# A recurrent kernel's head: rows of x turned by the array, input weights in chunks, biases loaded on all partitions

## The chip, the cores and the metric

The kernel runs on one core of one Trainium2 chip. A core has a matmul array with its weight loader (PE and PEld in the profile), VectorE (DVE), ScalarE (ACT), GpSimd (POOL) and a queue engine (SP), and 16 DMA engines that carry all its transfers. The metric is the device time of one execution in microseconds; all times below are microseconds unless marked otherwise.

## The reference

A gated recurrent layer over 128 steps of a batch of 64, with 512 inputs and 512 states, added to its input:

```
x: (64, 128, 512), h0: (64, 512)
Wz, Wr, Wh: (1024, 512)   # upper 512 rows meet x, lower 512 meet the state
Wp: (512, 512)

step t:
  z = sigmoid([x_t, h] @ Wz + bz)
  r = sigmoid([x_t, h] @ Wr + br)
  c = tanh([x_t, r * h] @ Wh + bh)
  h_new = (1 - z) * h + z * c
  y_t = h_new
  h = tanh(h_new @ Wp + bp)  if (t + 1) % 4 == 0 and t < 127  else h_new
out = x + y
```

All of it is in 32-bit floats.

## The kernel before

The work falls into two parts. The state part is serial: at each step the gates r, z and the candidate multiply the turned state (`hT`, `rhT`) by the state weights `wh[R]`, `wh[Z]`, `wh[H_]` (the lower halves), and at each fourth step by `wp`. The x part does not depend on the state: products of x with `wx`, the upper halves of the three weights. From step 4 on, the x part is computed for groups of four steps together by a scheme of fewer, pre-summed products (`batch`, with sums of weights in `tt`, `tw`, `d5`, `din` and sums of x in `s12r` and others); the first four steps are done one by one (`plain`).

A batch of 64 is handled as two halves of 32 (`h` = 0, 1). A product of one k (one of K = 4 blocks of 128 inputs) and one half is two matmuls of a 128x32 stationary tile against 256 columns (`products`, L222 is their matmul); a *unit* below is one k for both halves. Results of the x part gather in the PSUM tiles `scratch` q, r, a, x, y; `add_bias` (DVE, L437) adds the bias and writes `cp`, and `seed` (ScalarE, L398) copies `cp` into the PSUM of a gate (`rec`, `rec_z`) before the state's products are added there.

The order on each engine is the order in which the program issues the instructions; nothing reorders them. Two generators, `half(0)` and `half(1)`, walk over the steps, and a queue of x units fills the gaps between the gates (`fill`, with the numbers in `HEAD`, `PLACES`, `TAIL`). `both(n)` runs n units for both halves at once, `now` queues units and runs them.

The head stands before these generators. The array begins with idle matmuls on zeros (`idle`, L212). Meanwhile SP and ScalarE issue the loads: x of steps 0 to 3 in quarters (`load_step`, L112, pieces of 512 bytes), the input weights of r in two parts and of z and the candidate in one each (`load_wx`, L117), and later the state weights in quarters of 256 KB, each to 32 partitions, from both queues (`load_wh`, L98). x is turned by DVE (`join_x`, L264). The three biases come as rows through GpSimd's queue (L130), are spread over the partitions by matmuls against ones (`spread`, L194) and copied by ScalarE into `bias_x` (L202). GpSimd then waits on a copy `held` (L142), loads h0 (L144), forms the difference of the two halves of the biases (`bias_d`, L659), and begins the sums of weights (`sum_inner`, L318 to L321; `sum_outer`, L302 to L306). DVE does some of these sums itself (`sum_inner` of 1 and 2, `sum_outer_1` at L310), and turns h0 into `hT` (L251).

Each load takes a semaphore out of a small ring, so that a load waits, in the queue that issues it, for an earlier load that used the same semaphore; loads behind it in that queue wait too. GpSimd's loads have semaphores of their own.

Of the kernel before, what the change touches and what calls it, by code (L numbers as in the profile page):

```python
# [18 lines left out]
def kernel(  # L19
# [18 lines left out]
    S = 2  # L38
# [29 lines left out]
    ones = const.tile([1, V], F32, name="ones")  # L68
    nc.gpsimd.memset(ones, 1.0)
# [14 lines left out]
    bias_row = tw_all.rearrange("p a b -> p (a b)")[0:1, : 3 * H].rearrange("p (i n) -> p i n", i=3)  # L84
# [11 lines left out]
    def load_w(wt, w, k0=0, k1=K, engs=(nc.sync, nc.sync)):  # L96
        for q in (0, 2, 1, 3):
            engs[q // 2].dma_start(  # L98
                out=wt[part(q), k0:k1, :],
                in_=w[q * P + k0 * V : q * P + k1 * V, :].rearrange("(k e) n -> e k n", e=V),  # L100
            )
# [8 lines left out]
    def load_step(t, engs=both_queues):  # L110
        for q in (0, 2, 1, 3):
            engs[q // 2].dma_start(  # L112
# [3 lines left out]
    def load_wx(i, k0, k1):  # L116
        nc.sync.dma_start(  # L117
# [8 lines left out]
    load_step(0)  # L126
    load_wx(R, 0, 2)
    load_step(1, (nc.scalar, nc.scalar))
    for i, b in enumerate((br, bh, bz)):
        nc.gpsimd.dma_start(out=bias_row[:, i, :], in_=b.rearrange("(o n) -> o n", o=1))  # L130
    load_wx(R, 2, K)

    dummy = const.tile([1, 1], F32, name="dummy")
    nc.scalar.activation(dummy, ones[:, 0:1], AF.Sigmoid)

    for i in (Z, H_):
        load_wx(i, 0, K)

    for t in (2, 3):
        load_step(t, (nc.sync, nc.sync))  # L140
    held = const.tile([1, 1], F32, name="held")
    nc.gpsimd.tensor_copy(held, wx[0:1, 2, R, 0:1])  # L142
    for h in range(S):
# [3 lines left out]
        )  # L147

    def load_wh(i):
        load_w(wh[i], gates_in[i][D:], engs=both_queues)  # L150
# [39 lines left out]
    def spread(bank, rows, which):  # L190
        bank = bank.rearrange("p (i d j) -> p i d j", i=2, d=2)
        for h in range(S):
            for c in range(2):
                nc.tensor.matmul(  # L194
                    bank[part(2 * h + c), 0 : len(which)],
                    lhsT=ones,
                    rhs=quarters(bias_row[:, rows])[:, c],
                    start=True,
                    stop=True,
                )  # L200
        for j, i in enumerate(which):
            nc.scalar.copy(  # L202
                bias_x[:, :, :, i, :].rearrange("p n d u -> p d n u"),
                bank[:, j].rearrange("p d (n u) -> p d n u", n=C),
            )
# [52 lines left out]
    def join_x(g, i):  # L258
# [8 lines left out]
        )  # L267

# [160 lines left out]
    def banks(t):  # L429
        first, second = scratch[:2] if t % 2 == 0 else scratch[2:4]  # L430
        rooms = (first[:, : S * J], first[:, S * J :], second[:, : S * J])
# [11 lines left out]
    def plain_unit(t, e, k, start, end=None, gates=()):  # L443
# [4 lines left out]
        second = H_ if t == T - 1 else Z  # L448
# [554 lines left out]
```

## Time and profile before

| | |
|---|---|
| median of 3 runs | 1262.05 (1261.39 to 1263.48) |
| profiled execution | 1259.52, of which the span of the instructions 1257.6 |
| PE busy | 1250.6 (99%), 25960 matmul records |
| DVE, ACT, POOL busy | 805.5 (64%), 837.9 (67%), 891.5 (71%) |
| read from HBM, written to it | 40.11 MB, 16.78 MB |
| share of the 16 DMA engines in the first two slices of 31 us | 8 and 3 tenths |

Engine rows of the timeline give start, length, engine, line, operation, tiles written and read, and in brackets the idle time before with what ended it. A matmul of 32-bit floats is two records. In the chain of work each piece is what the end of the span was waiting for at that time. The row of a DMA issue gives the queue, the count, KB of each and the median time from issue to landing. Several matmuls of 32 columns run beside each other in the array, so the records' lengths overlap, and the time between starts counts.

### The profile page before, as it was taken

To read this page: it belongs to the slowest core of one execution; us is meant where nothing else is said; L and a number is where in the kernel's file an instruction comes from. 1 tells how busy PE (TensorE), PEld (TensorE's weight loads), DVE (VectorE), ACT (ScalarE), POOL (GpSimd) and SP (SyncE) were. 2 spreads that over 40 slices of the span, in tenths; PEclk is the share of its full clock that TensorE was granted. 3 is DMA by queue.
4 is the path that set the end of the run, shared out by engine and by line. 5 is a ranking of instruction groups with operands and counts; after the bars stand their busy time and mean duration, and the time that the engine had idled before them with its cause. 6 is when DMAs were issued, how large, how long until landed. Compare 5 with 4: busy or idle time off the path is not lost.

```text
span 1257.6 us, 60730 instructions
## 1 busy us (share of the span) xinstructions
PE 1250.6 (99%) x25960; PEld 1162.1 (92%) x25960; DVE 805.5 (64%) x2173; ACT 837.9 (67%) x2685; POOL 891.5 (71%) x1031
## 2 busy tenths in 40 slices
PE   9999999999999999999999999999999999999998
PEld 4899999999999999999999999999999999999975
DVE  4666666666666666666666666666666666666545
ACT  2566666767666666766666667667676666676665
POOL 3988877776876778767788676786777777677530
PEclk9999999999999999999999999999999999999999
DMA  8311112121121110211211111111111111111010
GB/s 240 91 28 45 49 41 53 36 54 39 34 53 48 41 47 26 53 53 37 53 29 43 53 43 47 38 47 41 53 37 49 40 37 53 42 48 37 9 42 23
DMA packets 113232, 60.82 MB, mean 48 GB/s; under 512 B 12836, under 2 KB 109348, under 8 KB 112964
## 3 DMA queue, kind: packets, MB, share of 16 engines
q1 hardware_dynamic: 111268, 55.00, 16.4%
q8 instruction: 205, 3.36, 1.1%
q10 hardware_dynamic: 1440, 1.80, 0.6%
q14 instruction: 63, 0.52, 0.1%
q0 software_dynamic: 256, 0.14, 0.1%
HBM read 40.11 MB, written 16.78 MB: 45 GB/s over the span
## 4 chain that ended last, share of the span: by engine, by line
PE 98%; DMA 1%; issue 1%; DVE 0%; SPq 0%; POOLq 0%; POOL 0%; ACT 0%; ACTq 0%
PE rec L222 44%; PE rec_z L222 16%; PE scratch_r L222 14%; PE scratch_q L222 11%; PE scratch_a L222 5%; PE scratch_x L222 4%; PE scratch_y L222 4%; DMA wx<-in_L_cond_Wr_dram 0%; SPq L821 0%; DMA xr<-in_x_dram 0%; DMA out_dram<-xr 0%; PE scratch_x L194 0%; DVE z L912 0%; POOLq L998 0%; POOL xr L811 0%
## 5 line engine op out<-in xcount | busy, mean ns | idle before, releaser
L222 PE MATMUL rec<-wh,rhT 128*32 128x256 f32 x4096 | 376.3, 379 | 0.0
L222 PE MATMUL rec<-wh,hT 128*32 128x256 f32 x3072 | 282.6, 379 | 0.0
L222 PE MATMUL rec_z<-wh,hT 128*32 128x256 f32 x3072 | 282.5, 379 | 0.0
L222 PEld LDWEIGHTS rec<-wh,rhT 128*32 128x32 f32 x4096 | 249.6, 110 | 21.1 <-ACT rec L398 1.2
L248 ACT ACTIVATE scratch_r<-rec 64x128 f32<-64x128 f32 x512 | 128.2, 250 | 138.3 <-PE rec L222 63.7
L398 ACT COPY rec<-cp 64x256 f32<-64x256 f32 x512 | 190.6, 372 | 19.9 <-DVE cp L437 0.4
L222 PEld LDWEIGHTS rec<-wh,hT 128*32 128x32 f32 x3072 | 187.4, 110 | 14.7 <-issue 1.8
L222 PEld LDWEIGHTS rec_z<-wh,hT 128*32 128x32 f32 x3072 | 193.8, 110 | 7.2
L248 ACT ACTIVATE rec_z<-rec_z 64x128 f32<-64x128 f32 x488 | 122.2, 250 | 90.1 <-PE rec_z L222 78.6
L248 ACT ACTIVATE c<-rec 64x128 f32<-64x128 f32 x512 | 139.7, 273 | 60.4 <-PE rec L222 48.8
L811 POOL TENSOR_TENSOR xr<-xr,h 128x256 f32<-128x256 f32 x127 | 93.2, 734 | 91.6 <-DVE h L925 91.6
L575 POOL TENSOR_TENSOR mb<-mb,mb 128x768 f32<-128x768 f32 x58 | 106.3, 1833 | 66.8 <-DVE mb L541 66.8
L575 POOL TENSOR_TENSOR cp<-mb,mb 128x768 f32<-128x768 f32 x76 | 139.2, 1831 | 9.5 <-DVE mb L541 5.8
L575 POOL TENSOR_TENSOR cp<-mb 128x768 f32<-128x768 f32 x46 | 84.2, 1831 | 57.0 <-ACT rec_z L398 55.5
L222 PE MATMUL scratch_r<-tw,s 128*32 128x192 f32 x928 | 120.9, 326 | 0.0
L514 ACT COPY cq<-scratch_q 128x384 f32<-128x384 f32 x212 | 102.1, 482 | 19.3 <-PE scratch_q L222 17.8
L531 DVE TENSOR_TENSOR cx<-scratch_r,cx 128x384 f32<-128x384 f32 x106 | 59.1, 558 | 84.1 <-PE scratch_r L222 66.8
L222 PE MATMUL scratch_q<-tt,s 128*32 128x192 f32 x928 | 103.7, 326 | 0.0
L873 DVE SCALAR_TENSOR_TENSOR keep<-rec_z,h 128x256 f32<-128x256 f32 x91 | 38.7, 425 | 95.6 <-ACT rec_z L248 94.6
L537 DVE TENSOR_TENSOR mb<-scratch_q,cx 128x384 f32<-128x384 f32 x106 | 59.1, 558 | 62.4 <-ACT cq L514 62.4
L853 DVE TENSOR_TENSOR rh<-scratch_r,h 128x128 f32<-128x128 f32 x192 | 56.1, 292 | 61.2 <-ACT scratch_r L248 61.2
L222 PE MATMUL rec<-wp,hT 128*32 128x256 f32 x992 | 91.5, 379 | 0.1
(188 smaller groups left out, 3846.5 us busy)
## 6 DMA issues: line engine op xcount, KB each, us to landing
out_dram<-xr SPq DMA_DIRECT2D x249, 64.0 KB, 1.8
xr<-in_x_dram SPq DMA_DIRECT2D x248, 64.0 KB, 2.1
xs<-in_x_dram SPq DMA_DIRECT2D x240, 64.0 KB, 2.0
wx<-in_L_cond_Wr_dram SPq DMA_DIRECT2D x2, 512.0 KB, 5.1
wx<-in_L_cond_Wz_dram SPq DMA_DIRECT2D x1, 1024.0 KB, 5.9
wx<-in_L_cond_Wh_dram SPq DMA_DIRECT2D x1, 1024.0 KB, 8.2
wp<-in_L_cond_Wp_dram SPq DMA_DIRECT2D x4, 256.0 KB, 5.3
wh<-in_L_cond_Wr_dram ACTq DMA_DIRECT2D x2, 256.0 KB, 3.8
```

Of the source, the lines that this page charges most:

```text
L222: nc.tensor.matmul(ps[part(2 * h + c)], lhsT=left, rhs=rhs(c), start=start, stop=True, skip_group_check=True,)
L248: nc.scalar.activation(dst[ts(d, 2 * V)], gate_ps(i, h)[ts(h, 2 * V), d, :], func)
L398: nc.scalar.copy(gate_ps(i, h)[rows].rearrange("p d (c n) -> p d c n", c=C), G[t][rows, :, :, i, :].rearrange("p c d n -> p d c n"),)
L514: nc.scalar.copy(c[:, :nm], ps[:, :nm])
L531: nc.vector.tensor_add(T2[what][:, :nm], r_ps[:, :nm], T2[what][:, :nm])
L537: nc.vector.tensor_add(blocks(1, 1), runs(q_ps[:, :nm]), runs(T2[what][:, :nm]))
L575: nc.gpsimd.tensor_add(dst, a, b)
L811: nc.gpsimd.tensor_add(xr[g][:, j], xr[g][:, j], h_new)
L853: nc.vector.tensor_mul(rh[:, h, :], r_, h_old[:, h, :])
L873: nc.vector.scalar_tensor_tensor(out=keep[:, part, :], in0=z_[:, part, :], scalar=1.0, in1=h_old[:, part, :], op0=ALU.subtract, op1=ALU.mult,)
```

## The change

- The array has an identity of 64x64 (`ident`, made by GpSimd). x of steps 0 and 1 is loaded as 64 rows of 2 KB (`load_rows`), turned by four transposes of the array for each step (`turn_rows`), and copied out of PSUM by DVE. The quarters of these two steps that the residual needs are loaded later, among the state weights of the candidate.
- r's input weights come in four loads of one k each (the first by ScalarE's queue), those of z and of the candidate in two each. The products of steps 0 and 1 are ordered so that each chunk of r is used for both steps when it is there; z's and the candidate's go by halves of k. The candidate's products of steps 0 and 1 get PSUM of their own (`scratch[4]`).
- The biases are loaded by twelve loads through GpSimd's queue directly to all partitions; the matmuls of `spread` are gone, `place_bias` is its copy by ScalarE. h0 comes between the biases of r and z. The copy `held` in front of them now waits for z's first half.
- The state weights are issued by SP alone, those of z with the quarters of x of step 3 between, those of the candidate with x of steps 0 and 1.
- 24 and 4 idle matmuls in place of 48; eight units ahead of step 0 in place of nine, with one more in step 0; on DVE `sum_outer_1` and the turn of x of step 3 stand ahead of the candidate's `add_bias`, and `bias_d` comes last on GpSimd before the sums; the turns of steps 4 and 5 and their sums move to the end of step 0.

```diff
-    def load_x(tile_, t0, n, j=0, engs=(nc.sync, nc.sync)):
-        for h in range(S):
-            for q in (0, 2, 1, 3):
-                engs[q // 2].dma_start(
+    def load_x(tile_, t0, n, j=0, hs=range(S), qs=(0, 2, 1, 3)):
+        for h in hs:
+            for q in qs:
+                nc.sync.dma_start(
...
-    load_step(0)
-    load_wx(R, 0, 2)
-    load_step(1, (nc.scalar, nc.scalar))
-    for i, b in enumerate((br, bh, bz)):
-        nc.gpsimd.dma_start(out=bias_row[:, i, :], in_=b.rearrange("(o n) -> o n", o=1))
-    load_wx(R, 2, K)
+    def load_rows(t, eng):
+        eng.dma_start(out=x_rows[:, ts(t, D)], in_=x[:, t, :])
+
+    load_rows(0, nc.sync)
+    load_wx(R, 0, 1, nc.scalar)
+    load_rows(1, nc.scalar)
+    for k in range(1, K):
+        load_wx(R, k, k + 1)
+    for k in (0, 2):
+        load_wx(Z, k, k + 2)
...
-    for i in (Z, H_):
-        load_wx(i, 0, K)
-
-    for t in (2, 3):
-        load_step(t, (nc.sync, nc.sync))
+    load_step(2)
+    for k in (0, 2):
+        load_wx(H_, k, k + 2)
     held = const.tile([1, 1], F32, name="held")
-    nc.gpsimd.tensor_copy(held, wx[0:1, 2, R, 0:1])
+    nc.gpsimd.tensor_copy(held, wx[0:1, 0, Z, 0:1])
+
+    def load_bias(i, b):
+        for q in range(NQ):
+            nc.gpsimd.dma_start(
+                out=bias_in[part(q), i],
+                in_=b.rearrange("(o d c j) -> c o d j", o=1, d=2, c=2)[q % 2].broadcast_to(
+                    [V, S, J]
+                ),
+            )
+
+    load_bias(R, br)
     for h in range(S):
         nc.gpsimd.dma_start(
             out=h_init[:, h, :],
             in_=h0[ts(h, V), :].rearrange("b (q j) -> q b j", q=NQ),
         )
+    load_bias(Z, bz)
+    load_bias(H_, bh)
...
+    def place_bias(i):
+        nc.scalar.copy(
+            bias_x[:, :, :, i, :].rearrange("p n d u -> p d n u"),
+            bias_in[:, i].rearrange("p d (n u) -> p d n u", n=C),
+        )
...
+    def turn_rows(t, bank):
+        if 0 not in xT:
+            xT[0] = xtp.tile([P, Q4, C, P], F32, tag="xT", name="xT_0")
+        for k in range(K):
+            nc.tensor.transpose(
+                bank[:, ts(k, B)],
+                x_rows[:, ts(t, D)].rearrange("b (p k) -> b k p", k=K)[:, k],
+                ident,
+            )
+        nc.vector.tensor_copy(xT[0][:, t].rearrange("p c n -> p (c n)"), bank[:, : K * B])
...
-    idle(48)
-    join_x(0, 0)
-    now(first[R][0])
-    join_x(0, 1)
-    now(first[R][1])
-    now(first[Z][0])
-    for i in (1, 2):
-        sum_inner(i, nc.vector, slice(0, 2))
-    spread(scratch[3], slice(0, 2), (R, H_))
+    idle(24)
+    turn_rows(0, scratch[4])
+    idle(4)
+    now(first[R][0][:1])
+    turn_rows(1, scratch[3])
+    for t, k in ((0, 1), (1, 0), (1, 1), (0, 2), (1, 2), (0, 3), (1, 3)):
+        now([first[R][t][k]])
+    for half_k in (slice(0, 2), slice(2, K)):
+        for t in range(2):
+            now(first[Z][t][half_k])
     load_wh(R)
-    now(first[Z][1])
+    for q in (0, 2, 1, 3):
+        load_step(3, (q,))
+        load_wh(Z, (q,))
+    for q in (0, 2, 1, 3):
+        load_x(xr[0], 0, 2, hs=(0,), qs=(q,))
+        load_wh(H_, (q,))
+    load_x(xr[0], 0, 2, hs=(1,))
+    sum_inner(1, nc.vector, slice(0, 2))
+    join_x(0, 2)
+    place_bias(R)
     for t in range(2):
         add_bias(t, (R,))
     for h in range(S):
         seed(R, 0, h)
-    spread(scratch[4], slice(2, 3), (Z,))
-    nc.gpsimd.tensor_sub(bias_d, bias_x[:, 1], bias0)
-    load_wh(Z)
+    sum_inner(2, nc.vector, slice(0, 2))
+    place_bias(Z)
     for t in range(2):
         add_bias(t, (Z,))
     seed(Z, 0, 0)
-    load_wh(H_)
-    join_x(0, 2)
     hT = new_T("hT", "hT_init")
     for h in range(S):
         turn(hT[:, h, :], h_init[:, h, :])
+    for half_k in (slice(0, 2), slice(2, K)):
+        for t in range(2):
+            now(first[H_][t][half_k])
+    sum_outer_1(nc.vector)
+    join_x(0, 3)
+    place_bias(H_)
+    for t in range(2):
+        add_bias(t, (H_,))
     for i in (1, 2):
         sum_inner(i, nc.vector, slice(2, 3))
-    now(sum(first[H_], []))
-    for t in range(2):
-        add_bias(t, (H_,))
-    join_x(0, 3)
-    sum_outer_1(nc.vector)
+    nc.gpsimd.tensor_sub(bias_d, bias_x[:, 1], bias0)
     nc.gpsimd.tensor_copy(held, d5[0:1, 1, 0, 0, 0:1])
...
-    both(9)
+    both(8)
...
         if t == 0:
+            join_x(1, 0)
+            join_x(1, 1)
+            sum_raw12(1)
             sum_outer(2)
             sum_outer(4)
...
-                yield from fill(2 * K - 3, h)
+                yield from fill(2 * K - 2, h)
...
-                if t == 0:
-                    join_x(1, 0)
-                    join_x(1, 1)
-                    sum_raw12(1)
```

More of the change, by code (lines that the diff above doesn't have):

```diff
@@ L67 @@
     nc.vector.memset(zeros, 0.0)
-    ones = const.tile([1, V], F32, name="ones")
-    nc.gpsimd.memset(ones, 1.0)
+    ident = const.tile([B, B], F32, name="ident")
+    make_identity(nc, ident)
     wx = const.tile([P, K, 3, H], F32, name="wx")
@@ L108, in new_xr, with load_step, load_wx @@
         xr[g] = xrp.tile([P, Q4, S, J], F32, tag="xr", name=f"xr_{g}")
-    def load_step(t, engs=both_queues):
-        for q in (0, 2, 1, 3):
-            engs[q // 2].dma_start(
+    def load_step(t, qs=(0, 2, 1, 3)):
+        for q in qs:
+            nc.sync.dma_start(
                 out=xr[0][part(q), t], in_=x[:, t, ts(q, J)].rearrange("(h b) u -> b h u", h=S)
             )
-    def load_wx(i, k0, k1):
-        nc.sync.dma_start(
+    def load_wx(i, k0, k1, eng=nc.sync):
+        eng.dma_start(
             out=wx[:, k0:k1, i, :],
@@ L188, in quarters @@
         return v.rearrange("p n (d c j) -> p c n d j", d=2, c=2)
[L190 to L205, printed above, removed]
+    def place_bias(i):
+        nc.scalar.copy(
+            bias_x[:, :, :, i, :].rearrange("p n d u -> p d n u"),
+            bias_in[:, i].rearrange("p d (n u) -> p d n u", n=C),
+        )
     bias0 = bias_x[:, 0]
@@ L430, in banks @@
         first, second = scratch[:2] if t % 2 == 0 else scratch[2:4]
+        if t < 2:
+            return first[:, : S * J], second[:, : S * J], scratch[4][:, ts(t, S * J)]
         rooms = (first[:, : S * J], first[:, S * J :], second[:, : S * J])
@@ L447, in plain_unit @@
             bank = (a_bank, x_banks[0], a_bank)
-        second = H_ if t == T - 1 else Z
+        second = H_ if t in (1, T - 1) else None if t == 0 else Z
         return (
```

18 lines of the change are left out of this document (11 added, 7 removed).

## The prediction

> **What bounds the kernel now.** I read the page's chain first, to see which engine sets the end.
>
> ```profile
> PE 98%; DMA 1%; issue 1%; DVE 0%; SPq 0%; POOLq 0%; POOL 0%; ACT 0%; ACTq 0%
> ```
>
> The array carries 98% of the way to the end; once it has begun its products it hardly waits. The change touches only the head and the order inside step 0. So the question is by how much the array reaches a given point behind the head earlier or later, and every later step keeps that shift. I read the head in the chain in order of time (start, length, what; x counts records, two to an instruction).
>
> ```profile
> 0.76 1.70 DMA xr<-in_x_dram
> 2.47 5.59 DMA wx<-in_L_cond_Wr_dram
> ...
> 8.11 1.07 PE scratch_q L222 x16
> ...
> 12.85 0.99 PE scratch_x L194 x8
> ...
> 15.70 0.56 PE scratch_y L194 x8
> ...
> 19.86 3.45 PE scratch_q L222 x64
> 23.31 0.43 PE scratch_a L222 x8
> 23.74 1.75 PE rec L222 x28
> ...
> 31.11 0.18 PE rec L222 x2
> ```
>
> Until 8.11 the chain is transfers: x, then r's second half of input weights. From then on it is the array: products of x, two blocks at L194 that spread the biases (0.99 and 0.56), gate r of step 0 from 23.74 and the candidate's gate from 31.11. One unit of products (one k, both halves of the batch) is 0.43, as 64 records in 3.45 show. Before gate r stand 24 units for steps 0 and 1 and nine more; afterwards eight more, and the ninth follows in step 0. So 23.31 is the moment to compare gate r with; for the candidate's gate, behind which the number of units is the same, it is 31.11.
>
> **The array alone.** What it could reach if nothing else held it:
>
> ```profile
> 1.20 1.04 PE L212 MATMUL rec<-zeros 128*32 128x512 bf16 x8 [1.20 <-DVE zeros L67]
> ...
> 6.46 1.07 PE L222 MATMUL scratch_q<-wx,xT 128*32 128x256 f32 x16
> ```
>
> 48 idle matmuls fill 1.20 to 6.4, 0.108 each, so 24 end at 3.8. The rows of x for step 0 (128 KB) should have landed: 32 KB took 1.70, 512 KB 5.59, and I take 2.3, that is 3.1. Four transposes are not in the trace. Eight instructions of products took 1.07 with their latency; half of that is 0.5, and four taken singly at 0.4 each are 1.6; I take 0.9, and 0.5 for a copy on DVE (0.41 is a row of the same 128x256 below). The first product then starts at 5.2. The second four transposes lie between products, at 0.7. 24 and 8 units are 13.8. That makes 19.7; some of the early products may wait for their chunk or run before the clock is up, so 20.2 (19.7 to 20.7), 3.1 before 23.31. The spread (1.55) is in this, the rest is the earlier start. r's four chunks hide: each feeds two units, and two units are 0.86.
>
> **The biases and hT.** On DVE, hT now stands behind the adds for r and z, and the sums d5 stand ahead of the turn of x of step 3.
>
> ```profile
> 17.99 0.46 DVE L251 STREAM_TRANSPOSE hT_init<-h_init 128x128 f32<-128x128 f32 x2
> ...
> 20.79 0.41 DVE L437 TENSOR_TENSOR cp<-scratch_x,bias_x 128x256 f32<-128x256 f32 x1
> 21.12 0.66 DVE L264 STREAM_TRANSPOSE xT<-xr 128x256 f32<-128x256 f32 x1
> 21.71 1.78 DVE L310 TENSOR_TENSOR d<-wx 128x768 f32<-128x768 f32 x2
> ```
>
> Twelve bias loads of 32 KB and two of h0 now go through GpSimd's queue, in the order r (4), h0 (2), z (4), candidate (4), behind a copy that waits for z's first half of input weights. hT therefore waits for the tenth of them. The nearest rows are the five loads of that queue before:
>
> ```profile
> 1.32 0.65 POOL L130 DMA_DIRECT2D tw<-in_L_cond_br_dram  x1 [0.46 <-issue]
> ...
> 2.47 0.49 POOL L130 DMA_DIRECT2D tw<-in_L_cond_bz_dram  x1
> ...
> 23.78 0.99 POOL L318 TENSOR_TENSOR tt<-wx 128x384 f32<-128x384 f32 x1
> ```
>
> ```profile
> wh<-in_L_cond_Wh_dram SPq DMA_DIRECT2D x2, 256.0 KB, 8.9
> ...
> h_init<-in_cond_dram POOLq DMA_DIRECT2D x2, 64.0 KB, 6.2
> ...
> tw<-in_L_cond_br_dram POOLq DMA_DIRECT2D x1, 2.0 KB, 3.4
> tw<-in_L_cond_bh_dram POOLq DMA_DIRECT2D x1, 2.0 KB, 4.5
> tw<-in_L_cond_bz_dram POOLq DMA_DIRECT2D x1, 2.0 KB, 5.4
> ```
>
> From issue to landing they took 3.4 to 6.2; I take 4.6, in the middle. Issued 0.5 to 0.65 after each other, the three rows landed at 4.7, 6.5 and 7.9, so 1.4 to 1.8 apart behind long loads of input weights. The interval of the new ones lies between 0.5 (GpSimd's issue) and 1.8. I take 0.85, because the state weights come in quarters of 256 KB, with 32 and 64 KB pieces of x between, where the three rows waited behind halves of 512 KB. z's first half lands after 1.84 MB, about 7.2 by the rates below. So the first bias lands at 11.8, the tenth at 11.8 + 9 x 0.85 = 19.5, the last at 22.9.
>
> The Trainium skill, DMA: Bandwidth & Descriptors, section Queues, rings and completion order, states that a DMA engine goes round its queues and drains a whole packet, typically 9 to 17 descriptors, from one before it turns to the next. By that rule each bias load waits for one packet of SP's queue; a quarter of a state weight has 8 rows of 2 KB on each engine, and the estimate for its turn is about 1 us, with which the tenth would land at 20.8 and the sum below would come out at no gain. The spacing of the three rows agrees with such turns.
>
> From 19.5: ScalarE's copy 0.4, two adds 0.75 with their overlap, the two turns 0.46, a semaphore 0.15, so hT at 21.25. DVE then needs 1.78 and 0.66, which gives x of step 3 at 23.8 with 0.1 between. The array starts gate r at 21.3, has 1.75 of it and comes to the ninth unit at 23.1: it stands 0.7. Before, the ninth unit in that place would have begun at 23.31 + 1.75 = 25.06. The gain by this way is 25.06 - 23.9 = 1.15.
>
> GpSimd's own chain of sums began at 23.78. Now it begins behind the difference of two biases (0.99 for such a row), at 22.9 + 0.4 + 1.0 = 24.3; I see no wait of the array on it before, and 0.5 should stay hidden. Moving the turns of group 1's x and the four sums of its first two steps behind step 0 costs nothing while the array's next units read older tiles; if that cover is gone, a late GpSimd is the second rival below.
>
> **The state weights.** The candidate's gate needs all of its state weights.
>
> ```profile
> 19.43 1.55 SPq L98 DMA_DIRECT2D wh<-in_L_cond_Wh_dram  x2
> ```
>
> ```profile
> 4.50:12.50 8.00, 7.35 (x116) 3.37 (x108) 3.23 (x7) 0.58 (x2) 1.52 (x3) 1.00 1.05 388
> 13.50:15.20 1.70, 1.70 (x32) 0.92 (x32) 0.71 (x2) 0.86 (x3) 0.00 (x0) 1.00 0.36 75
> 15.20:29.00 13.80, 13.80 (x255) 8.01 (x249) 8.91 (x25) 3.77 (x12) 6.14 (x8) 1.00 1.05 252
> 36.40:41.20 4.80, 4.80 (x106) 3.39 (x102) 2.31 (x7) 2.75 (x11) 4.80 (x6) 1.00 0.96 243
> ```
>
> (The last two columns are the DMA engines' share and GB/s.) The last quarter was issued near 20.4 and landed 8.9 later, 29.3: that is 1.8 ahead of the gate. The engines were full before it but for 13.50 to 15.20, where SP and ScalarE had issued too little; with SP issuing all weights ahead of that, 64% of 1.7, 1.1, comes back. New ahead of it are 0.39 MB of biases and 0.26 MB of x for the residual (half of that load stands in front), 0.65 MB at 252 GB/s, 2.6. The rows of x in place of the short pieces give back between 0 and 1.3 (its 0.26 MB was part of the slow 5.59); I take 0.9. So 29.3 + 2.6 - 1.1 - 0.9 = 29.9, and the gate starts 1.15 earlier than 31.11. One queue instead of two costs nothing here by the last row: Wp came through SP alone at 243 GB/s, the state weights through both at 252.
>
> **The sum.** The array alone would gain 3.1, hT's way 1.15, the weights' way 1.15; the latest ends last, so 1.1 is gained. The profiled execution took 1259.52 with a span of 1257.6, and would take 1258.4; it lies 2.5 below the median of 1262.05, from which the forecast is 1260.9.
>
> **The rivals.** (1) Only the array counts: the biases land 0.5 apart, so the tenth is there by 16.3, and the rows of x bring the weights forward by all of 1.3 and more. For it: the idle stretch before 15.20 and 0.5 as GpSimd's issue time. Against it: the engines at 1.05 until 29. It gains 3.1 and gives 1259.0.
> (2) Slower: GpSimd's queue is late. With the spacing of the three rows, 1.4, the tenth bias lands at 24.4 and the last at 30.0. The ninth unit starts at 28.7 instead of 25.06, 3.6 late. GpSimd's sums start at 31.4 instead of 23.78, 7.6 late, and what the array reads of them first is late by something between; I take 4.5 in all, 1266.5. It decides as soon as the tenth bias lands after 20.6, at a spacing of 0.98. For it: those three rows. Against it: their neighbours were twice as long.
> (3) Also slower: quarters that write the same 32 partitions from one queue come at four fifths of the rate of two. 3.1 MB at 252 GB/s are 12.5; a quarter more is 3.1, less the 1.1 gained: 1264.1 or a little more. Against it stands the row of Wp.
>
> **How the numbers follow.** The measurement can tell about 0.2%, 2.5 us, from no change. The forecast has 0.43, from 1259.3 to 1262.5 by the bounds above; a fifth of it lies below 1259.5. Rival 1 has 0.28, nearly all below 1259.5; rival 2 0.23, nearly all above 1264.6; rival 3 0.06, half of it above. So faster 0.36, slower 0.26, the same 0.38. The range leaves out the ends of rivals 1 and 2: 1258.6 to 1266.2. The forecast's own is 1259.3 to 1262.5.
>
> **What would show it.** In the changed kernel's chain the first product of step 0 should stand near 5.2, gate r near 21.3 with a short stand of the array before the ninth unit that ends with DVE's turn of x, and the candidate's gate near 30.0, released by a load of its state weights. GpSimd's loads should land from 11.8 to 22.9. Gate r at 20.2 without a wait means rival 1; ScalarE waiting for bias loads until after 22, with DVE and the array behind it, rival 2; quarters of weights more than 1.1 apart with DMA engines short of full, rival 3. A product at half speed behind the transposes, or a wait after step 1, would be a cost that I have not counted.

## The result, and the profile after

The changed kernel takes 1270.52 us (median of 6), the kernel before 1260.55 (median of 6; the forecast started from the median of the first three of them, 1262.05): a ratio of 1.0077, with a 95% interval from 1.0057 to 1.0097. It is 10 us slower, where a gain of 1.1 was forecast (1260.9), and it lies beyond the end of the range, 1266.2. The six runs fall into two groups, 1268.28 to 1268.87 and 1272.17 to 1272.78, and the profiled execution, 1272.54, is of the upper one, so a shift read from its trace can be larger than the one of the medians.

From the page of the changed kernel, the span and the chain's shares:

```profile
span 1270.1 us, 60706 instructions
...
PE 90%; POOL 4%; DMA 2%; SPq 1%; issue 1%; DVE 0%; ACT 0%; POOLq 0%; ACTq 0%
```

The array still carries the end, but with 90% in place of 98%: GpSimd and transfers have come in. Its head, from the chain in order of time (start, length, what):

```profile
3.01 7.45 DMA wx<-in_L_cond_Wz_dram
...
10.51 0.12 POOL held L150
10.63 6.96 DMA tw<-in_L_cond_br_dram
...
17.87 0.53 POOL tw L154
18.40 8.13 DMA tw<-in_L_cond_bz_dram
...
26.59 0.41 ACT bias_x L212
...
27.03 0.44 DVE cp L460
...
27.49 0.39 ACT rec_z L419
...
28.10 3.07 PE rec L232 x26
```

And on GpSimd, behind the first eight loads:

```profile
17.87 1.06 POOL L154 DMA_DIRECT2D tw<-in_L_cond_bz_dram  x2 [2.47 <-DMA tw<-in_L_cond_br_dram]
```

This is one line of cause from the first transfers to gate r of step 0: z's first half of input weights (lands at 10.46), GpSimd's copy that waited for it, the first bias, a later bias load that GpSimd could issue only when that first one had landed (17.59), the landing of z's bias at 26.53, its copy, the add, the seed of gate z (beside it VectorE turns h0 into `hT`, from 27.70 on), and the array at 28.10. With the moment to compare of before, 23.31, that is 4.8 late (5.0 by the starts in the timelines, 23.13 and 28.10), and the array's own work is not in the line at all. What the array waited for, in total (us, times, longest):

```profile
PE rec L232 <- ACT rec_z L419: 3.7, 1, 3.7
PE rec L232 <- ACT scratch_r L258: 3.0, 1, 3.0
PE scratch_y L283 <- DMA x_rows<-in_x_dram: 1.9, 1, 1.9
...
PE scratch_q L232 <- DVE mb L560: 0.8, 1, 0.8
PE scratch_x L232 <- POOL s12r L352: 0.5, 1, 0.5
```

Four places: gate r (the biases), the candidate's gate (gate r's result), the rows of x, and late sums of GpSimd and VectorE in the first steps (a wait of 0.5 for the adds of r's bias and one of 0.3 for a sum are left out above). Before had 1.2 for the zeros and 0.6 for r's weights, and nothing else. The timeline of the array, with the wait in brackets:

```profile
5.89 0.71 PE L283 MATMUL scratch_y<-ident,x_rows 64*128 64x64 f32 x4 [1.94 <-DMA x_rows<-in_x_dram]
...
7.12 1.08 PE L232 MATMUL scratch_q<-wx,xT 128*32 128x256 f32 x8
...
11.95 0.60 PE L232 MATMUL scratch_a<-wx,xT 128*32 128x256 f32 x8
...
40.70 0.41 PE L232 MATMUL rec<-wh,rhT 128*32 128x256 f32 x2 [2.95 <-ACT scratch_r L258]
```

The rows of step 0 land late, the first product starts at 7.12, and eight records take 1.08 there and 0.60 only from 11.95 on: until then the array works at half its rate. It did so already ahead of the stand. Eight idle products in the changed kernel, and eight in e13, a run described below:

```profile
2.46 1.07 PE L222 MATMUL rec<-zeros 128*32 128x512 bf16 x8
```

```profile
4.50 0.60 PE L212 MATMUL rec<-zeros 128*32 128x512 bf16 x8
```

From start to start these eight take 0.85 and 0.43. In e13 the array came to its full rate at about 4.0, in the changed kernel, with the stand in between, only between 11.4 and 11.7. Behind the longer stand, at gate r, it falls back to half, as the windows show (last three columns: granted clock, DMA share, GB/s):

```profile
24.40:28.10 3.70, 0.04 (x4) 0.03 (x1) 1.07 (x4) 0.78 (x2) 0.00 (x0) 1.00 1.09 226
28.10:32.20 4.10, 4.10 (x42) 2.52 (x45) 4.07 (x8) 1.27 (x4) 2.28 (x4) 0.58 1.06 232
32.20:36.00 3.80, 3.80 (x76) 2.65 (x72) 3.77 (x4) 0.37 (x1) 3.72 (x4) 1.00 0.51 120
```

After 3.66 without work, the granted clock is 0.58 over 4.1 us; it is 0.50 from 28.73 to 32.14. And the candidate's gate at 40.70 is not released by a load of weights, as the forecast had it, but by gate r's result, which VectorE had put behind eight sums for the candidate. These sums beside GpSimd's (the first two of each, from both timelines of the changed kernel):

```profile
31.01 1.04 DVE L339 TENSOR_TENSOR tt<-wx 128x128 f32<-128x128 f32 x1
32.09 1.04 DVE L340 TENSOR_TENSOR tt<-tt,wx 128x128 f32<-128x128 f32 x1
...
30.92 0.99 POOL L339 TENSOR_TENSOR tt<-wx 128x384 f32<-128x384 f32 x1
31.98 1.00 POOL L340 TENSOR_TENSOR tt<-tt,wx 128x384 f32<-128x384 f32 x1
```

and the first of the same sums in before, where GpSimd was not yet at work:

```profile
18.38 0.25 DVE L318 TENSOR_TENSOR tt<-wx 128x128 f32<-128x128 f32 x1
```

A sum a third as large as GpSimd's takes as long as GpSimd's, 1.04 in place of 0.25 to 0.29, and starts and ends about 0.1 behind it. In the profiled execution the candidate's gate is 9.8 late (40.70 against 30.90): 5.0 at gate r, about 1.7 by 3.41 us at half the clock, and 2.95 for gate r's result.

### The profile page after: what moved, and what is told of

It is laid out like the page before. It is cut to its first block, busy times and chain, and to the rows that moved or that the text cites. A ratio compares the mean times of both kernels' runs of the same rounds, so it can differ in the third digit from the quotient of the medians.

```text
span 1270.1 us, 60706 instructions
## 1 busy us (share of the span) xinstructions
PE 1252.6 (99%) x25932; PEld 1157.7 (91%) x25932; DVE 810.8 (64%) x2173; ACT 836.3 (66%) x2685; POOL 896.0 (71%) x1041
## 4 chain that ended last, share of the span: by engine, by line
PE 90%; POOL 4%; DMA 2%; SPq 1%; issue 1%; DVE 0%; ACT 0%; POOLq 0%; ACTq 0%
PE rec L232 42%; PE rec_z L232 15%; PE scratch_r L232 12%; PE scratch_q L232 10%; PE scratch_a L232 5%; PE scratch_y L232 4%; PE scratch_x L232 4%; POOL cp L598 1%; POOL mb L603 1%; DMA tw<-in_L_cond_bz_dram 1%; DMA wx<-in_L_cond_Wz_dram 1%; DMA tw<-in_L_cond_br_dram 1%; SPq L858 1%; POOL xr L848 0%; SPq L94 0%
```

## The experiments

Times are medians, beside before's 1260.05 (e1 to e4), 1260.08 (e5 to e7), 1260.00 (e8 to e11), 1259.89 (e12, e13), 1260.61 (e14) and 1260.50 (e15). In brackets is the interval of the ratio.

### What the changed kernel pays for its biases

**e1**: the changed kernel with VectorE's sums moved.

```
     sum_inner(2, nc.vector, slice(0, 2))
+    for i in (1, 2):
+        sum_inner(i, nc.vector, slice(2, 3))
     place_bias(Z)
...
-    for i in (1, 2):
-        sum_inner(i, nc.vector, slice(2, 3))
     nc.gpsimd.tensor_sub(bias_d, bias_x[:, 1], bias0)
```

> The changed kernel with one block moved: the eight DVE sums of the candidate's weights stand ahead of z's add instead of behind the candidate's. Theory 1 (the tenth bias load delays gate r to 28.1, and then DVE's eight sums run at GpSimd's pace, 8.3 instead of 2.2, and hold the candidate's gate): the sums take about 0.28 each again, because GpSimd is idle there; the reset state is turned near 32.5; the array no longer stands 2.95 before the candidate's gate, which starts near 37.7 instead of 40.70; gate r stays at 28.1; 3 to 4 less than the changed kernel's 1270.5, so 1267. Theory 2 (the last quarter of the state weights, at 34.0, and the later loads of x hold everything): 1270.5, within 1.

Measured: 1268.21, [1.0043, 1.0073]. Gate r starts at 28.21, as without the edit; the candidate's gate comes at 36.67 in place of 40.70, and the wait for gate r's result is gone. The span falls by 4.2 (1265.9), the median, counted over before, by 1.8. The array and a sum on VectorE in e1:

```profile
28.21 1.92 PE L232 MATMUL rec<-wh,hT_init 128*32 128x256 f32 x24 [3.37 <-DVE hT_init L261]
...
36.67 0.39 PE L232 MATMUL rec<-wh,rhT 128*32 128x256 f32 x2
...
22.95 0.28 DVE L339 TENSOR_TENSOR tt<-wx 128x128 f32<-128x128 f32 x1
```

Of the 4.0 at the candidate's gate, 2.95 are the stand for the sums. The other 1.1 comes from the array: behind its stand at gate r it goes on at the full rate here (24 records in 1.92; the changed kernel took 3.07 for 26).

**e2**: the changed kernel, GpSimd let go only behind VectorE's last sum.

```
-    nc.gpsimd.tensor_copy(held, d5[0:1, 1, 0, 0, 0:1])
+    nc.gpsimd.tensor_copy(held, din[0:1, 1, 0, 2, 0:1])
```

> The changed kernel, with GpSimd's copy in front of its sums waiting for DVE's last sum of the candidate's weights instead of d5; the order on DVE is unchanged. Theory 1: the eight DVE sums, in the same place, take 0.28 each and 2.2 together instead of 8.3, because GpSimd is not summing beside them; the candidate's gate starts near 37.7; GpSimd's sums start 2.4 later, hidden behind its later wait for x of step 4; 1267 to 1268. If the sums are slow for another reason (transfers, the array), they stay near 1.05 each, and GpSimd's later start makes it 1271 to 1274.

Measured: 1268.14, [1.0044, 1.0074]; VectorE's sums take 0.28 to 0.34 each.

```profile
27.11 3.47 PE L232 MATMUL rec<-wh,hT_init 128*32 128x256 f32 x28 [2.60 <-ACT rec_z L419]
...
36.44 0.40 PE L232 MATMUL rec<-wh,rhT 128*32 128x256 f32 x2
```

Here the order on VectorE is untouched and only GpSimd's start is moved, and the sums are as fast as in e1. So it is the two engines side by side that makes the sums slow. The stand for them, 2.95 in the changed kernel's trace, is gone in both runs. The candidate's gate comes 4 us earlier in both, but about 1 of it is something else: the full rate in e1, and in e2 gate r, which starts 1.0 earlier.

**e3**: the changed kernel with the three biases loaded as rows at the start and spread by the array, as in before, into `rec[1]` and `rec[2]`.

```
-    load_bias(R, br)      # and of Z, H_; place_bias too
+    for i, b in enumerate((br, bh, bz)):
+        nc.gpsimd.dma_start(out=bias_row[:, i, :], in_=b...)      # ahead of held
...
             now(first[Z][t][half_k])
+    spread(rec[1], slice(0, 2), (R, H_))
+    spread(rec[2], slice(2, 3), (Z,))
```

> The changed kernel with the biases as before: three rows loaded at the start and spread by matmuls (into the gates' PSUM), h0 alone behind the copy that waits for z's first half. Theory 1: hT waits only for h0, about 18.5, gate r starts when the array comes to it, near 25 with the 1.6 of spread; the sums of the candidate's weights still run beside GpSimd's, so the reset state is turned near 33 to 34, and the candidate's gate starts near 34; 6 less than 1270.5, so 1264 to 1265. Theory 2 (state weights): with 0.39 MB less in front they land near 32.5, and the gain would be 1.5 at most, 1269.

Measured: 1268.39, [1.0039, 1.0080]; gate r at 25.79, the candidate's gate at 35.31 behind a stand of 1.58 for gate r's result: the slow sums again.

**e4**: the edits of e1 and e3 together.

> The last two edits together: biases as rows and spread, and the candidate's sums ahead of z's add. Theory 1: the candidate's gate starts where the array comes to it (near 32.4) or where the last quarter of its weights lands (near 32.5); 7.5 to 8.5 less than 1270.5, so 1262 to 1263: what remains above the kernel before is the transfers. Theory 2: the same as with the rows alone. If it comes out below 1260.5, the transfers cost nothing.

Measured: 1263.63, [1.0016, 1.0036]; gate r at 24.55, the candidate's gate at 32.58 without a wait. Of the 10 us, 6.4 go with the two edits together, where each alone took 1.6 to 1.8: as long as one of the two holds the candidate's gate, the other hides in part. 3.6 are left. The array's waits in e4 name some of them:

```profile
PE scratch_y L303 <- DMA x_rows<-in_x_dram: 1.9, 1, 1.9
...
PE scratch_q L252 <- DVE mb L580: 0.8, 1, 0.8
PE scratch_x L252 <- POOL s4r L372: 0.4, 1, 0.4
PE scratch_x L252 <- POOL s12r L372: 0.4, 1, 0.4
```

### The parts of the change put into the kernel before, one at a time

**e5**: before with the twelve bias loads by GpSimd behind its first `held` (r, h0, z, candidate), each placed by ScalarE ahead of its adds, and no spread.

```
-    spread(scratch[3], slice(0, 2), (R, H_))
+    place_bias(R)
...
-    spread(scratch[4], slice(2, 3), (Z,))
+    place_bias(Z)
```

> The kernel before with the bias part alone: twelve loads to all partitions through GpSimd's queue, behind the same copy as before (r's second half of input weights, 8.1), h0 between those of r and z, copies by ScalarE, the difference of the biases last; the candidate's sums stay ahead of its add. Theory 1: the tenth load lands 13 to 16 after the copy, near 22 to 24, so hT at 24 to 26 and gate r 1 to 3 later than 23.7; the candidate's sums are not beside GpSimd's; slower than before by 1 to 4: 1262 to 1264.5. If the bias loads cost nothing by themselves: 1259, by the spread that is gone.

Measured: 1263.67, [1.0023, 1.0051], 3.6 over before and within what was expected, though gate r comes later than that, at 27.74. It saves the spread's 1.55 of the array and is slower all the same:

```profile
20.50 5.35 PE L224 MATMUL scratch_q<-wx,xT 128*32 128x256 f32 x64 [2.35 <-DVE xT L266]
```

VectorE's turn of step 2's x stands behind the adds of z's bias, and comes late with them; the array stands 2.35, and its next 64 records take 5.35 where in before the same row has 3.64.

**e6**: before with the state weights by SP alone.

```
-        load_w(wh[i], gates_in[i][D:], engs=both_queues)
+        load_w(wh[i], gates_in[i][D:])
```

> The kernel before with the state weights issued by SP alone, nothing else changed. Theory 1: SP issues r's first quarter behind x of step 3, near 14.5, where ScalarE issued two at 13.9 and 14.6, so all land up to 1 later, which the 1.8 in front of the candidate's gate hides: 1260.5, within 1. Theory 2 (one queue carries 32-partition quarters more slowly): the last lands 3 or more later, the array stands before the candidate's gate: 1262 to 1264.

Measured: 1259.82, [0.9986, 1.0005]: one queue instead of two is free.

**e7**: before with x of steps 0 and 1 as rows turned by the array, r's weights in four loads, and the change's idle products; the eight pieces of x for the residual are loaded behind the state weights.

```
-    idle(48)
-    join_x(0, 0)
-    now(first[R][0])
+    idle(24)
+    turn_rows(0, scratch[4])
+    idle(4)
+    now(first[R][0][:1])      # and on as in the change
...
     load_wh(H_)
+    load_x(xr[0], 0, 2)
```

> The kernel before with the x part alone: rows of x of steps 0 and 1 turned by the array, r's input weights in four loads used chunk by chunk, 24 and 4 idle matmuls; z's and the candidate's loads, the biases, the state weights and the order behind stay as before, and x for the residual follows the state weights. Theory 1: the first product starts near 7, a second chunk near 9, so the array gains at most 1 on the kernel before, whose products began at 6.5 and went on at 8.1: 1259.5 to 1261. If rows and chunks bring the early start that was forecast (5.2): 1258.

Measured: 1266.12, [1.0029, 1.0059], the worst of the parts, and more than either theory had. Up to the candidate's gate it loses 1.6 (32.48 against 30.90). The rest is in step 0, on VectorE:

```profile
37.98 1.14 DVE L274 STREAM_TRANSPOSE xT<-xr 128x256 f32<-128x256 f32 x2 [4.56 <-DMA xs<-in_x_dram]
```

The turns of `xr_1` wait 4.56 for loads that now stand behind the residual's eight on SP; behind them on VectorE stands the new state, and the array waits 3.2 for `hT`. The move of these turns behind step 0 in the change avoids just this.

**e9**: e7 with that move.

```
         if t == 0:
+            join_x(1, 0)
+            join_x(1, 1)
+            sum_raw12(1)
             sum_outer(2)
...
-                if t == 0:
-                    join_x(1, 0)
-                    join_x(1, 1)
-                    sum_raw12(1)
```

> The kernel of e7 (before, with x of steps 0 and 1 as rows and r's weights in four loads) with the two joins of xr1 and the sum behind them moved to the end of step 0, as the changed kernel has them. Theory: e7's loss of 6 us was 1.6 from the rows and the rest from the join that waits 4.56 us for its loads; with the joins at the end of step 0 that wait goes, the array doesn't stand 3.2 us for hT any more, gate r of step 1 comes at 36.5 to 37 in place of 40.1, and the time is 1.6 to 2.5 us above before: 1261.7 to 1262.6 where before is 1260.1. Rival: the rows cost the rest by themselves (loads of x pushed back on SP): the time stays above 1264.5.

Measured: 1263.91, [1.0017, 1.0037]. The stand for `hT` is gone and 2.1 us with it (counted over before), but not all that was expected: 3.9 over before are left. In its profile the array keeps half its rate for longer than in e7 (for the first 48 records of products behind the transposes, against some 24), which is 1.2: the trace's record of the granted clock begins, at full, at 12.90 in e9 and at 10.31 in e7, with the same program up to there. What sets that moment stays open.

**e10**: before with only that move (the diff of e9).

> The kernel before with only the two joins of xr1 and the sum behind them moved from step 0's candidate to the end of step 0. The changed kernel and the one of e4 lose another 2 us or so between step 1 and before's 101 us, which the one with only the biases doesn't. Theory: it is the moved joins, which make the first pairs of GpSimd's sums late: the candidate's gate of step 0 stays at 30.9, and the time is 1 to 2.5 us above before. Rival: the joins are free there, the time is within 1 us of before, and the loss comes from the later loads of xr1 behind the eight loads of x added on SP's queue.

Measured: 1262.23, [1.0007, 1.0025]: the move alone costs 2.2. Three rows of its array's waits, 1.6 together, are the ones that e4 and the changed kernel show:

```profile
PE scratch_q L222 <- DVE mb L537: 0.8, 1, 0.8
...
PE scratch_x L222 <- POOL s4r L331: 0.4, 1, 0.4
PE scratch_x L222 <- POOL s12r L331: 0.4, 1, 0.4
```

GpSimd's first pair of sums starts at 39.29 in place of 35.55, and the products that read it come before it is there. Its profile loses another 0.7 ahead of the candidate's gate to a late load, which the edit doesn't touch; whether that belongs to the edit stays open.

### Mending the head

**e8**: the changed kernel with GpSimd let go earlier.

```
-    nc.gpsimd.tensor_copy(held, wx[0:1, 0, Z, 0:1])
+    nc.gpsimd.tensor_copy(held, wx[0:1, 0, R, 0:1])
```

> The changed kernel with one edit: GpSimd is let go by the first chunk of r's input weights (landed at 4.85 us) and not by z's first half (10.46). Nothing else is touched, so VectorE's last sums still stand beside GpSimd's. If the late release is what makes the biases late (theory): r's four land near 14 to 15 in place of 17.6 to 19.8, the last bias near 25 in place of 29.25, gate r's first product near 25 in place of 28.1, the candidate's gate near 37.5 in place of 40.7, and the time falls by 2 to 3 us to about 1267 on a chip where the changed kernel takes 1269 to 1270. If the loads' own pace decides and the release is hidden behind it (rival: they lie behind the weights in the 16 engines, and from the ninth on each waits for a landing): the last bias lands at 28 or later, gate r's first product stays at 27.5 or later, and the time changes by less than 1 us. The early issue can also take DMA time from the chunks of r: then the first product comes later than 7.1.

Measured: 1272.21, [1.0073, 1.0102], no better than the changed kernel, though the span of its profiled execution is 2.5 shorter. That execution, 1269.39, is the shortest of four, and no trace shows the other three, 1272.07 to 1272.83. Yet the biases came as the theory had it. ScalarE's copies of the three, then the array:

```profile
13.28 0.41 ACT L212 COPY bias_x<-tw 128x256 f32<-128x256 f32 x1 [10.01 <-DMA tw<-in_L_cond_br_dram]
19.11 0.41 ACT L212 COPY bias_x<-tw 128x256 f32<-128x256 f32 x1 [3.86 <-DMA tw<-in_L_cond_bz_dram]
23.11 0.40 ACT L212 COPY bias_x<-tw 128x256 f32<-128x256 f32 x1 [2.73 <-DMA tw<-in_L_cond_bh_dram]
...
28.16 0.41 PE L232 MATMUL scratch_a<-wx,xT 128*32 128x256 f32 x2 [2.28 <-DVE xT L274]
38.21 0.41 PE L232 MATMUL rec<-wh,rhT 128*32 128x256 f32 x2 [2.12 <-ACT scratch_r L258]
```

The copies stand 6 to 7.5 earlier, gate r starts at 23.98, and then the array stands 2.28 for step 3's x, which VectorE can turn only at 27.47 behind its load, and 2.12 behind the slow sums. One wait gone, the next in its place: both theories fall, since the loads moved and the time didn't.

**e12**: the edits of e8 and e1, and step 3's x ahead of all state weights.

```
+    load_step(3)
     load_wh(R)
-    for q in (0, 2, 1, 3):
-        load_step(3, (q,))
-        load_wh(Z, (q,))
+    load_wh(Z)
```

> The changed kernel with three edits: GpSimd let go by the first chunk of r's weights (as in e8), VectorE's sums for the candidate ahead of z's bias (as in e1), and step 3's four quarters of x loaded ahead of all state weights. In e8 the biases came in time, and the array then waited 2.3 us for step 3's x and 2.1 us for gate r's result behind VectorE's slow sums. Theory (the biases by GpSimd cost nothing in themselves, only the release, the sums and the order of loads do): both waits go, the candidate's gate comes at 32 to 33.5 as in e4, and the time is as in e4, 1263 to 1265 where before is 1260. Rival (twelve loads of biases cost DMA time that the state weights lack, whenever they are issued): the last state weights land at 33 or later, the candidate's gate comes after 34.5, and the time stays above 1266.

Measured: 1265.08, [1.0022, 1.0048], between the theories and nearer to the first. The array's stands for biases, sums and step 3's x are gone; new are 1.04 for the candidate's input weights and 0.49 for ScalarE, and the candidate's gate comes at 33.97, 1.4 behind e4's. The twelve loads can be had in time, but the rows with the spread remain 1.6 cheaper.

**e15**: e4 with more idle products, `idle(42)` in place of `idle(24)`.

> The kernel of e4 (the changed kernel with the biases as rows spread by the array and VectorE's sums ahead) with one number changed: 42 idle products in place of 24, so that they end near 5.75, when step 0's rows land. In e4 the array stands 1.89 us before the first transposes, and the eight products behind take 1.08 us where before's rate is 0.43 per eight; only from 10.9 on are they at full rate. Theory: it is the stand that halves the array's rate there; with 42 idle products the stand goes, the first product still starts near 7, and the first sixteen units come 1.2 to 1.6 us sooner, so gate r's first product at 23.0 to 23.4 in place of 24.55 and the time 1.2 to 1.6 us lower, 1262.0 to 1262.5. Rival (the transposes themselves, or the wait for chunks, slow the first products): eight products behind the transposes still take about 1.0 us, gate r's first product stays at 24.2 or later, and the time stays within 0.5 of 1263.6.

Measured: 1263.93, [1.0018, 1.0036], the same as e4. The mechanism is as expected, and nothing is left of it at the end:

```profile
7.05 0.64 PE L252 MATMUL scratch_q<-wx,xT 128*32 128x256 f32 x8 [0.19 <-DVE xT L308]
...
26.49 0.41 PE L252 MATMUL scratch_a<-wx,xT 128*32 128x256 f32 x2 [1.23 <-DVE xT L294]
```

With idle products up to the transposes the products behind them run at the full rate (the trace's record of the full clock begins at 5.54, in e4 at 10.50), and gate r starts at 23.36, 1.2 earlier; then the array waits 1.23 for step 3's x.

### Trying to beat both

**e11**: before with r's weights in four loads used chunk by chunk, x by quarters, step 1's x ahead of the second chunk, 40 idle products.

```
-    load_wx(R, 0, 2)
-    load_step(1, (nc.scalar, nc.scalar))
+    load_wx(R, 0, 1)
+    load_step(1)
...
-    load_wx(R, 2, K)
+    for k in range(1, K):
+        load_wx(R, k, k + 1)
```

> The kernel before with r's input weights in four loads used chunk by chunk, but x of steps 0 and 1 loaded by quarters and turned by VectorE as before, step 1's quarters issued half by SP ahead of the second chunk, and 40 idle products in place of 48. Theory: the array is the bound throughout before, so what its first product gains reaches the end: first product at 5.5 to 5.9 in place of 6.43 and the wait of 0.6 for the second half of r's weights gone, 0.6 to 1.4 us in all, 1258.7 to 1259.5 where before is 1260.1. Rival: the bytes set the pace, so the array waits as long later on (step 1's quarters, the chunks): within 0.3 us of before. Slower rival: the waits at the chunks pull the granted clock down and cost more than they give: above 1261.

Measured: 1262.25, [1.0008, 1.0025].

```profile
5.58 0.64 PE L223 MATMUL scratch_q<-wx,xT 128*32 128x256 f32 x8
7.73 0.64 PE L223 MATMUL scratch_q<-wx,xT 128*32 128x256 f32 x8 [1.52 <-DMA wx<-in_L_cond_Wr_dram]
...
13.23 1.93 PE L223 MATMUL scratch_q<-wx,xT 128*32 128x256 f32 x32 [2.27 <-DMA wx<-in_L_cond_Wz_dram]
```

The first product is 0.9 earlier and the array stands 3.8 behind it: z's weights land at 13.19 in place of 10.49. They were issued at 5.28 in place of 4.59 and took 7.9 in place of 5.9: from 8 to 10 the engines moved 215 GB/s, in before 409. Why they moved so little with z's and the candidate's weights issued is not shown.

**e13**: before with the spread of r's and the candidate's biases between r's second and third chunk for step 0.

```
-    now(first[R][0])
+    now(first[R][0][:2])
+    spread(scratch[3], slice(0, 2), (R, H_))
+    now(first[R][0][2:])
...
-    spread(scratch[3], slice(0, 2), (R, H_))
```

> The kernel before with one move: the spread of r's and the candidate's biases (eight matmuls, 1.0 us) stands between the first two and the last two chunks of r for step 0, where the array waits 0.57 us for the second half of r's weights. Theory: the array is the bound, so the 0.57 us that it now stands is filled, all later work comes 0.5 to 0.6 us sooner, and the time falls by as much, 1259.4 to 1259.5 where before is 1260.0, at the edge of what can be told; the wait for Wr of 0.6 is gone from the array's waits. Rival: the candidate's bias (landed 6.49 in before) comes late in this queue, or the state weights take over as the bound: within 0.2 us of before.

Measured: 1262.53, [1.0011, 1.0028]. It fills its wait and loses more:

```profile
8.61 0.34 ACTq L98 DMA_DIRECT2D wh<-in_L_cond_Wr_dram  x1
8.99 0.55 ACTq L98 DMA_DIRECT2D wh<-in_L_cond_Wr_dram  x1
...
17.48 3.58 PE L222 MATMUL scratch_r<-wx,xT 128*32 128x256 f32 x32 [2.20 <-DMA wx<-in_L_cond_Wh_dram]
```

ScalarE, done early with the biases, issues state weights at 8.6 that in before it issued at 13.9, and the candidate's input weights land at 17.44 in place of 13.48.

**e14**: e13 with the state weights by SP alone (the diff of e6).

> The kernel of e13 with one edit more: all state weights are loaded by SP, as in e6. In e13 ScalarE, done with the biases early, sent two quarters of r's state weights at 8.6 and 9.0 us (in before 13.9 and later), the candidate's input weights landed at 17.4 in place of 13.5, and the array waited 2.2 us for them. SP sends its loads in the order of the program, behind step 3's x. Theory: with that the candidate's input weights land at 13.5 to 13.9 again, the wait of 2.2 goes, and the 0.57 us filled by the spread is left as a gain: 1259.3 to 1259.6 where before is 1260.0, by the profile a first product of gate r at 22.7 to 23.1 in place of 23.56 in before. Rival (something else than ScalarE's early loads made e13 late): the candidate's input weights land after 16 and the time stays above 1262.

Measured: 1260.12 against 1260.61, [0.9986, 1.0004]: as before. The candidate's input weights land at 14.88 and the array no longer waits for them, so ScalarE's early loads were what made e13 late. Of the expected gain nothing can be told: gate r comes at 23.57 behind a wait of 0.62 for its own state weights, which are the next bound. No version here beats the kernel before.

## Why the prediction was wrong

**The state weights by one queue** was right: free, as e6 shows; rival 3 falls.

**The array alone** failed at its first term. The rows of x were taken to land 2.3 after issue, at 3.1; they landed after 5.0, at 5.8, with r's first chunk (4.85) and the second rows (6.80) under way beside them. Between 4 and 6 us, 207 GB/s were moved; that these three loads held one another up is likely, but no run loads the rows alone. The first product came at 7.12 and not at 5.2. The half rate behind the transposes was named in the prediction as a cost not counted: the first 40 records of products, from 7.12 to 11.95, take 2.0 more than at 0.43 for eight. e15 shows that the transposes are not its reason: 24 idle products and a stand of 1.94 behind them left the array at the half rate with which it had begun. So the 32 units, done by 20.2 in the forecast (19.7 and an allowance of 0.5), ended at 24.4: 1.9 by the start, 2.0 by the rate, 0.5 by a wait for r's bias, and some tenths more.

**The biases and hT**, the way that set the forecast, had the right links and three sizes too small. What was named as rival 2's sign (0.23) came: ScalarE waited for bias loads until 26.5, DVE and the array behind it. But rival 2 had it by a spacing of 1.4 between the loads, and the spacing was 0.99; most came from the release and the first landing. GpSimd was let go at 10.46 and not at 7.2, as the 1.84 MB ahead came slower: 3.3. The first load then took 7.0 and not 4.6: 2.4. From the first to the tenth it took 8.9 and not 7.65: 1.3. The sum is the 7.0 by which z's bias came later, 26.5 against 19.5. For the last term the trace shows a wait that was overlooked: GpSimd's loads have eight semaphores, so the ninth, z's third, was issued 2.47 late, when the first had landed; how much of the 1.3 is due to it is not shown. Rival 2's own figure of 24.4 for the tenth was still 2.1 too early. The estimate of about 1 us a load by the Trainium skill's round of packets (DMA: Bandwidth & Descriptors, section Queues, rings and completion order) comes out as a mean, 8.9 over nine. The runs don't show the rule itself: single spacings go from 0.45 to 2.40, and in e5 the same nine took 5.25.

**The sums of VectorE** were not costed at all. The prediction doesn't name the eight sums for the candidate (`din`), which the change moves behind the candidate's adds, and so counts neither their place ahead of gate r's result nor what they would meet there. They cost 2.95 at the candidate's gate. GpSimd's sums start at 30.92, VectorE's at 31.01, and eight sums take 8.3 in place of 2.2. The Trainium skill states the rule, in SBUF — State Buffer, section SBUF: two separate sides: VectorE shares a pair of ports with GpSimd when its instruction reads two inputs from SBUF, and whichever comes first holds it for a whole instruction. By that rule each of VectorE's sums waits out one of GpSimd's; the trace agrees (1.04 beside 1.00), and e1 and e2 take the cost away from either side.

**The moved turns and sums of group 1** were costed at nothing "while the array's next units read older tiles", and a late GpSimd was left to rival 2. The cover doesn't hold: e10 measures 2.2, with the array waiting for sums of GpSimd that start 3.7 later.

**The state weights' way** was not what decided: the last quarter landed at 34.0 and not at 29.9, behind engines that were full until 32.2, but the candidate's gate had other waits ahead of it until e4.

**The sum** took the latest of three ways. That was sound as far as it goes; the mistakes were that the sizes in two of them were too small, that a stand can cost more than its length and that the chain behind the head (sums, group 1) was not carried on. Measured over before: 2.2 for the moved turns (e10), 1.7 for the rows (e9 less e10), and 3.6 for the biases alone (e5). From the other end, e4 has 3.6 left, so 6.4 of the 10 go with the biases and VectorE's sums, and 1.4 beside the moved turns are for the rows and all else. The rest of the change, the halves of z's and the candidate's input weights and the order of their products above all, was not tried alone.

## What to carry to other kernels

Before an array that never waits, everything that is moved off it must arrive in time: ask of each moved load what lets it go, how many can be under way, and what it takes from the loads behind it; and of each moved operation, what runs beside it at its new place. A wait taken away is worth only the distance to the next one, as e8, e14 and e15 show: three times a mechanism was right and the time stayed where it was. Undoing one part of a change and doing one part alone give different sums; both are needed.

## What the runs showed of the hardware

- VectorE's sums of two operands in SBUF go at GpSimd's pace beside GpSimd's sums: 1.04 in place of 0.28 us.
- The array begins at half its rate and comes to the full one at a time that differs between runs. The trace's record of the granted clock begins, at full, at 3.96 in e13, 5.54 in e15, 6.15 in before, 10.50 in e4 and 11.66 in the changed kernel, and the rows of the array get short there. Ahead of it the windows read 1.00 all the same, as from 7 to 11 in the changed kernel, where eight records took 1.08.
- Behind some stands the granted clock is 0.50, and each time for 3.41 us: from 28.73 in the changed kernel, 26.86 in e2, 21.20 in e5, 41.03 in e7, 29.36 in e8 and 17.61 in e13. These moments lie 17.07, 13.65, 17.07, 30.72, 17.07 and 13.65 behind the first full clock of their runs, which are 5, 4, 5, 9, 5 and 4 times 3.41. Cut into stretches of 3.41 from the first full clock on, the runs sort themselves: the array stood 2.20 or more in the stretch just ahead of each of the six falls (2.20 in e13, 2.79 in the changed kernel), and at most 2.03 in any other. So a stand of 3.37 in e1, which lies across two stretches (2.01 and 1.49), and one of 2.27 in e11 (1.00 and 1.27) cost only their length, while 2.20 in e13 and 2.35 in e5 cost more (32 records in 3.58 for 1.9; 64 in 5.35 for 3.64). The Trainium skill, TensorE: Matmul & The Clock Gate, section Part 1: The HAM clock gate, tells of a free-running window of about 3.4 us; the length and the spacing of these falls agree with it.
- A load let go early can be the reason for a late one elsewhere: two quarters of 256 KB issued 5 us sooner made a load of 1 MB land 4 us later (e13).
